# Causal score tiles in pairs, values of 17 columns and second projection buffers in a decoder kernel

## The chip, the cores and the metric

The kernel is one program on one core of a Trainium2 chip. Its time is the device time of one execution in microseconds. Five engines work side by side, each on its own queue of instructions: PE (TensorE, matmuls), DVE (VectorE), ACT (ScalarE), POOL (GpSimd) and SP (SyncE, which issues most DMAs here). "PEld" in the profile is PE's loading of weights.

## The reference, cut to what matters

Four sequences of 512 rows of 256 values go through two decoder layers. Each layer is attention, cross-attention to a context of 1601 rows, and a feed-forward part, each followed by a residual and a layer norm. The second layer is where the change lies: 16 heads of 16 values, causal self-attention with rotated queries and keys, and cross-attention without a mask.

```python
q, k = apply_rope(x @ wq + bq), apply_rope(x @ wk + bk)     # 16 heads of 16
scores = einsum('bnqh,bnkh->bnqk', q, k) / 4
attn = softmax(where(tril, scores, -inf))                   # 512 x 512, causal
x = layernorm(x + einsum('bnqk,bnkh->bnqh', attn, v) @ wo + bo)
x = layernorm(x + cross_attention(x, ctx_512))              # 512 x 1601, no mask
x = layernorm(x + tree_ffn(x))                              # 255 gates, 256 leaves
```

## The kernel before

The program has three stages. `front` makes the first layer's attention and cross-attention, `experts` its sorted mixture of experts, and `heads` the whole second layer. `front` and `experts` end at about 500 us in the profile; the change touches `heads` alone (from line 901 on).

The order of the instructions inside a stage is not written by hand. The stage adds nodes to a `Plan`: each node has an engine, a planned cost, a place in an order (`prio`), the nodes that it depends on, the pool of buffers that it takes one from, and those that it frees. `Plan.run` then picks, over and over, the node that can start earliest by the planned costs, and issues its instructions. So a changed cost or a changed number of buffers moves instructions on every engine, though the chip's own times differ from the planned ones. Matmul nodes carry a mode, `row`, `col` or `full`, and `Plan.turn` tries to keep nodes of one mode together.

In `heads` the work goes by head groups: four heads at a time, four groups per sequence, four sequences, first all of the self-attention and then all of the cross-attention, overlapped by the planner. A group takes these steps:

- `projections` makes queries and keys of eight heads (two groups). For self-attention it also rotates them in `rope`: a product with the rotation matrix, a DVE multiplication into a buffer `rt`, and two POOL operations into `qu` or `ku`. There is one `rt`, one `qu` and one `ku`.
- `apart` copies `qu` and `ku` by eight DMAs into `qT` and `kT`, so that each head lies at its own 32 partitions (lane). A score matmul then uses 32 rows of the array, and four heads can use the four lanes.
- Pass 1 (`score`, `largest`) makes the scores query-major, one tile of 128 queries at a time, and takes each row's maximum on DVE straight out of PSUM. In self-attention tile kq has (kq + 1) x 128 columns, because of the causal mask, and each tile has a PSUM bank of its own (`one`, seven of them).
- The maxima are negated, transposed by PE (`turn`) and added to the queries (`qa`).
- Pass 2 (`score`, `weigh`) makes the scores key-major: key tile t against the queries from t x 128 on. ACT takes Exp from PSUM to an SBUF buffer (`pe`, ten of them); in self-attention POOL then clears the upper triangle (`causal`).
- `product` multiplies by the values, four heads in four column groups of the array, into one bank `acc`. The values `VV` hold 32 columns per head: 16 values, a column of ones that gives the softmax sum, and 15 zeros.

At the start of the stage `begin` gathers the rows that `experts` left in DRAM (four indirect DMAs by POOL for each sequence) and norms them. Before that POOL clears `nm` and `qT` (`clear`), and after the first gathers it writes zeros and ones into `VV` (`ones_behind`). SP meanwhile loads the weights of the tree and fills the three `kT` buffers from `keys0`. The helper `mm` records its matmuls under line 239, so the profile tells the groups apart by their tiles: `one<-kT,qT` is pass 1, `one<-qa,kT` pass 2, and line 1188 the product with the values. Line 1113 is the causal maximum, 1109 that of cross-attention, 1173 Exp, and 1179 the triangle.

Of the kernel before, what the change touches and what calls it, by code (L numbers as in the profile page):

```python
# [29 lines left out]
NS = 31  # L30
NF = 24
# [171 lines left out]
def tile_decoder(ctx: ExitStack, tc: tile.TileContext, a, out):  # L203
# [697 lines left out]
    def heads():  # L901
        plan = Plan()
        with tc.tile_pool(name="h1", bufs=1) as h1, \
# [12 lines left out]
            VV = slots("v", 2, [P, NKT, H // 2, 32])  # L916
# [9 lines left out]
            Q0, RT = slots("q0", 2, [P, L]), slots("rt", 1, [P, L])  # L926
            QU, KU = slots("qu", 1, [P, L]), slots("ku", 1, [P, LC])

            plan.pool("f", 6)
            FF = [*Q0, *RT, junk, *(h1.tile([P, L], F32, tag=f"f{i}", name=f"f{i}") for i in range(2))]  # L930
# [11 lines left out]
            def ones_behind(n, t):  # L942
                nc.gpsimd.memset(t[:, :, :, HD:], 0.0)
                nc.gpsimd.memset(t[:, :, :, HD : HD + 1], 1.0)
# [3 lines left out]

            cleared = N("pool", 1.5, -1.5, clear)
            keyed = [N("dma", 2.5, -4.0, None, [N("sp", 0.4, -4.0, lambda n, k=k: key_rows(n, k))]) for k in range(3)]  # L950
            framed = [N("pool", 5.0, -1.5 + k, lambda n, k=k: ones_behind(n, VV[k])) for k in range(2)]


# [106 lines left out]
            def head_group(cross, b, g, pos, vals, pair, after):  # L1060
# [15 lines left out]
                qd = N("sp", 1.6, pr, lambda n: apart(QT, q, QU, qu, L), [q, cleared, *qs])  # L1076
                qready = N("dma", 0.5, pr, None, [qd], free=[qu])
                kd = N("sp", 1.6, pr, lambda n: apart(KT, k, KU, ku, nk), [k, *keyed, *ks])
# [10 lines left out]
                else:  # L1089
                    for kq in range(4):  # L1090
                        units += [(j, 0, [(kq, 0, (kq + 1) * P)]) for j in range(4)]
                maxes, scored = [], []
                for i, (j, m, prods) in enumerate(units):
                    pu = pos - 1.2 + (i + 0.5) / len(units)
                    js = slice(32 * j, 32 * j + 32)
                    nn, w = len(prods), prods[0][2] - prods[0][1]

                    def score(n, prods=prods, js=js, w=w):
                        for i, (kq, k0, k1) in enumerate(prods):
                            mm(ONE[n.slot][:, i * w : (i + 1) * w], QT[q.slot][js, kq * P : (kq + 1) * P],  # L1100
                               KT[k.slot][js, k0:k1])

                    s = N("pe", cost_mm(nn * w), pu, score, [mx], take=["one"], lanes=(j,), mode="row")

                    def largest(n, s=s, j=j, m=m, prods=prods, w=w):
                        nn, kq = len(prods), prods[0][0]
                        t = ONE[s.slot][:, : nn * w]
                        if cross:
                            nc.vector.tensor_reduce(  # L1109
                                MX[mx.slot][:, kq : kq + nn, j, m : m + 1], t.rearrange("p (a n) -> p a n", a=nn),  # L1110
                                AX.X, ALU.max)
                        else:
                            nc.vector.tensor_tensor_reduce(  # L1113
                                out=junk[:, :w], in0=t, in1=m_qk[:, 384 - kq * P : 512],
                                scale=1.0, scalar=NEG, op0=ALU.add, op1=ALU.max,
                                accum_out=MX[mx.slot][:, kq, j, 0:1])

                    maxes.append(N("dve", dve(nn * w), pu, largest, [s], free=[s]))
                    scored.append(s)
# [38 lines left out]
                for t in range(nkt):  # L1158
                    kn = kt_size(t) if cross else P
                    q0 = 0 if cross else t * P  # L1160
                    exps = []
                    for i, j in enumerate((2, 3, 0, 1)):
                        pu = pos + (t + 0.25 * i) / nkt
                        js = slice(32 * j, 32 * j + 32)
                        w = hold("pe", pu, [acc])
# [349 lines left out]
```

## Time and profile before

| | |
|---|---|
| median of 3 runs | 1765.67 us (1763.68 to 1767.53) |
| profiled execution, its own time | 1755.73 us |
| its span, first to last instruction | 1754.0 us |
| mean granted TensorE clock | 0.967 |
| PE busy, matmuls | 1661.4 us, 10756 records |
| DVE, ACT, POOL busy | 1110.2, 761.5, 342.3 us |

The page gives the busy time of each engine as a share of the span, then the span in 40 slices of 44 us with one digit for each (tenths of the slice), and the granted clock of PE and the load of the DMA engines in the same slices. Below stand the chain of work that ended last, followed back from the last instruction, and the costliest groups of instructions: line, engine, operation, written and read tiles, shape, count, busy time and mean duration. A shape like 32*128 ahead of a matmul's operands is the part of the array that it uses. A matmul in fp32 leaves two records, one for each pass. The profiled execution was 9.94 us shorter than the median of the runs.

### The profile page before, as it was taken

How to read it: one execution, taken by the hardware profiler on the slowest of the kernel's cores; microseconds unless marked ns; L12 is line 12 of the kernel's file. 1: busy time of each engine (PE TensorE's matmuls, PEld its weight loads, DVE VectorE, ACT ScalarE, POOL GpSimd, SP SyncE). 2: the span in 40 equal slices, each digit the busy share in tenths (PEclk: the TensorE clock that was granted, in tenths of full speed). 3: DMA queues.
4: the chain of work that ended last, by engine and by line, in shares of the span. 5: the costliest groups of instructions: out<-in, count | busy, mean ns of one | idle time of the engine just before them, and what ended most of it. 6: DMA issues, size and time to landing. Idle time of an engine off the chain costs nothing.

```text
span 1754.0 us, 28495 instructions
## 1 busy us (share of the span) xinstructions
PE 1661.4 (95%) x10756; PEld 862.5 (49%) x10756; DVE 1110.2 (63%) x2678; ACT 761.5 (43%) x1593; POOL 342.3 (20%) x521
## 2 busy tenths in 40 slices
PE   7899988999968999999999999999999999999995
PEld 4677775887754444454433334433334333343323
DVE  6997654121237766667776666777667776677625
ACT  0335551211112334444355555456554555545581
POOL 6652003432134534442100000100001000010000
PEclk9999987999988989999999999999999999999998
DMA  9000006876431100001100000001000010001000
GB/s 304 29 4 10 13 26 220 290 238 207 144 108 37 32 10 16 13 19 21 24 1 13 14 14 13 1 13 26 13 14 1 13 26 13 14 1 25 1 1 12
DMA packets 40843, 87.50 MB, mean 50 GB/s; under 512 B 7808, under 2 KB 26752, under 8 KB 37632
## 3 DMA queue, kind: packets, MB, share of 16 engines
q1 hardware_dynamic: 31728, 42.58, 9.0%
q0 software_dynamic: 8832, 43.00, 7.1%
q8 instruction: 86, 1.41, 0.3%
q14 instruction: 53, 0.43, 0.1%
q10 hardware_dynamic: 144, 0.07, 0.0%
HBM read 64.52 MB, written 8.26 MB: 41 GB/s over the span
## 4 chain that ended last, share of the span: by engine, by line
PE 83%; DVE 11%; DMA 2%; issue 2%; ACT 1%; POOL 1%; DVEq 0%; POOLq 0%; SPq 0%; ACTq 0%
PE one L239 53%; PE acc L1188 14%; PE e_one L239 11%; DVE junk L1113 1%; PE one L563 1%; PE one L1147 1%; PE one L1208 1%; DMA xs<-x_dram,tok 1%; PE one L1270 1%; DMA y<-ys_dram,dest 1%; DVE sc L423 1%; DVE pm L528 0%; ACT pe L1173 0%; DVE pr L462 0%; DVE qk L406 0%
## 5 line engine op out<-in xcount | busy, mean ns | idle before, releaser
L1173 ACT ACTIVATE pe<-one 128x512 f32<-128x512 f32 (+4 forms) x1088 | 533.0, 566 | 385.9 <-PE one L239 382.1
L1109 DVE TENSOR_REDUCE mx<-one 128x1 f32<-128x512 f32 x768 | 487.7, 683 | 182.1 <-PE one L239 178.3
L239 PE MATMUL one<-qa,kT 32*128 32x512 f32 (+4 forms) x2176 | 512.6, 600 | 7.7 <-ACT pe L1173 6.3
L239 PE MATMUL one<-kT,qT 32*128 32x512 f32 (+4 forms) x2560 | 500.7, 536 | 8.0 <-DVE mx L1113 2.6
L239 PEld LDWEIGHTS one<-qa,kT 32*128 32x128 f32 (+1 forms) x2176 | 171.8, 182 | 227.8 <-issue 78.0
L1188 PE MATMUL acc<-pe,v 128*32 128x512 f32 (+4 forms) x2176 | 270.7, 569 | 0.0
L239 PEld LDWEIGHTS one<-kT,qT 32*128 32x128 f32 x2560 | 191.5, 185 | 153.8 <-ACT pe L1173 45.3
L1276 POOL TENSOR_TENSOR x<-x,rows 128x1024 f32<-128x1024 f32 x12 | 28.3, 2356 | 802.4 <-PE one L1270 802.4
L1113 DVE CUSTOM_DVE_ANT_0 junk<-one,consts 128x256 f32<-128x256 f32 (+3 forms) x256 | 125.4, 490 | 50.7 <-PE one L239 25.8
L1188 PEld LDWEIGHTS acc<-pe,v 128*32 128x32 f32 (+1 forms) x2176 | 43.9, 108 | 178.6 <-issue 161.9
L1179 POOL TENSOR_SCALAR_AFFINE_SELECT pe<-pe 128x128 f32<-128x128 f32 x256 | 72.5, 298 | 140.9 <-ACT pe L1173 137.3
L239 PEld LDWEIGHTS e_one<-xsT,wgu 128*128 128x128 f32 x768 | 90.7, 194 | 4.8 <-issue 3.8
L239 PE MATMUL e_one<-xsT,wgu 128*128 128x128 f32 x768 | 90.6, 277 | 0.0
L239 PE MATMUL e_one<-xT,w_sgu 128*128 128x512 f32 x128 | 61.8, 624 | 3.1 <-DMA w_sgu<-in_w_shared_gu 3.1
L239 PE MATMUL one<-w_in,xT 128*128 128x512 f32 (+1 forms) x128 | 49.5, 543 | 10.4 <-DMA xT<-in_xT 10.4
L243 ACT COPY o<-acc 128x512 f32<-128x512 f32 x32 | 18.7, 586 | 75.5 <-PE acc L1188 75.5
L239 PE MATMUL one<-ctxT,q 128*128 128x512 f32 (+1 forms) x128 | 49.5, 518 | 0.0
L544 ACT ACTIVATE pe<-one,nm 128x512 f32<-128x512 f32 x64 | 37.3, 596 | 27.8 <-DVE nm L536 27.7
L239 PE MATMUL one<-pT,ctxN 128*128 128x128 f32 (+1 forms) x416 | 49.0, 275 | 0.0
L239 PEld LDWEIGHTS one<-pT,ctxN 128*128 128x128 f32 (+1 forms) x416 | 48.2, 192 | 1.6 <-issue 1.2
L852 DVE TENSOR_TENSOR he<-sg,e_one 128x512 f32<-128x512 f32 x24 | 16.5, 686 | 50.7 <-PE e_one L239 48.1
L830 DVE TENSOR_SCALAR xs<-xs,scs 128x256 f32<-128x256 f32 x24 | 8.5, 364 | 60.3 <-DMA xs<-x_dram,tok 60.3
(261 smaller groups left out, 1866.2 us busy)
## 6 DMA issues: line engine op xcount, KB each, us to landing
kT<-ku SPq DMA_DIRECT2D x64, 100.1 KB, 3.4
qT<-qu SPq DMA_DIRECT2D x128, 32.0 KB, 1.9
ctxN<-in_ctxN SPq DMA_DIRECT2D x4, 832.0 KB, 8.9
ctxT<-in_ctxT SPq DMA_DIRECT2D x4, 800.5 KB, 9.5
ys_dram<-ye SPq DMA_DIRECT2D x24, 128.0 KB, 2.4
kT<-in_keys SPq DMA_DIRECT2D x3, 800.5 KB, 9.7
xT<-in_xT SPq DMA_DIRECT2D x16, 128.0 KB, 3.6
x<-in_x SPq DMA_DIRECT2D x16, 128.0 KB, 6.0
```

Source lines behind the costliest of these rows:

```text
L239: nc.tensor.matmul(out, lhsT, rhs, start=c == 0, stop=c == n - 1)
L243: nc.scalar.copy(dst, src)
L423: scores.append(N("dve", 1.21, pos + 0.22 + 0.05 * s, lambda n, s=s, pr=pr: nc.vector.tensor_reduce(SC[sc.slot][:, s].rearrange("p t h -> ...
L544: nc.scalar.activation(PE_[w.slot][:, : k1 - k0], ONE[b.slot][:, : k1 - k0], AF.Exp, bias=NM[nm.slot][:, 1:2], accum_out=PS[sm_.slot][:, i ...
L563: nc.tensor.transpose(ONE[n.slot][:kn, (t % 4) * P : (t % 4 + 1) * P], PE_[w.slot][:, (t % 4) * P : (t % 4) * P + kn], ident)
L1109: nc.vector.tensor_reduce(MX[mx.slot][:, kq : kq + nn, j, m : m + 1], t.rearrange("p (a n) -> p a n", a=nn), AX.X, ALU.max)
L1113: nc.vector.tensor_tensor_reduce(out=junk[:, :w], in0=t, in1=m_qk[:, 384 - kq * P : 512], scale=1.0, scalar=NEG, op0=ALU.add, op1=ALU.max, ...
L1147: nc.tensor.transpose(ONE[n.slot][:, kq * P : (kq + 1) * P], NM[nm.slot][:, kq].rearrange("p j r -> p (j r)"), ident)
L1173: nc.scalar.activation(PE_[w.slot][:kn, q0:], ONE[s.slot][:kn, q0:], AF.Exp, scale=HD**-0.5)
L1179: nc.gpsimd.affine_select(d, d, pattern=[[1, P]], compare_op=ALU.is_ge, fill=0.0, base=0, channel_multiplier=-1)
L1188: nc.tensor.matmul(ACC[acc.slot][32 * j : 32 * j + 32, q0:], VV[v.slot][:kn, t, 4 * (g % 2) + j, :], PE_[exps[j ^ 2][0].slot][:kn, q0:], s ...
L1276: rw = N("pool", pool(1024), pos, lambda n: nc.gpsimd.tensor_tensor(XB[b], XB[b], rows[:, row : row + D].unsqueeze(1).to_broadcast([P, 4, ...
```

## The change

Four things are edited, all in `heads`.

- In self-attention two score tiles go into one PSUM bank. Pass 1 takes the query tiles in the order 3, then 0 and 2 together (128 + 384 columns), then 1. Pass 2 takes the key tiles in the order 0, then 1 and 3 together (384 + 128 columns), then 2. One Exp reads both tiles of a bank and writes one `pe` buffer; the maxima and the triangles are still taken tile by tile.
- The values have 17 columns per head instead of 32, and the product writes 17 partitions of each column group. `acc` is cleared once by DVE at the start of the stage, and POOL no longer writes zeros into `VV`.
- `rt`, `qu` and `ku` have two buffers each. The tree's pool `f` keeps its six buffers: the second `rt` takes the place of one.
- `clear` and `ones_behind` depend on the four gathers of the first sequence. The planned cost of `apart` on SP is 2.7 instead of 1.6, that of `ones_behind` 0.4 instead of 5.0.

```diff
 NS = 31
+MQ = (3,), (0, 2), (1,)
+TQ = (0,), (1, 3), (2,)
 NF = 24
...
-            VV = slots("v", 2, [P, NKT, H // 2, 32])
+            VV = slots("v", 2, [P, NKT, H // 2, HD + 1])
...
-            Q0, RT = slots("q0", 2, [P, L]), slots("rt", 1, [P, L])
-            QU, KU = slots("qu", 1, [P, L]), slots("ku", 1, [P, LC])
+            Q0, RT = slots("q0", 2, [P, L]), slots("rt", 2, [P, L])
+            QU, KU = slots("qu", 2, [P, L]), slots("ku", 2, [P, LC])
 
             plan.pool("f", 6)
-            FF = [*Q0, *RT, junk, *(h1.tile([P, L], F32, tag=f"f{i}", name=f"f{i}") for i in range(2))]
+            FF = [*Q0, *RT, junk, h1.tile([P, L], F32, tag="f0", name="f0")]
...
             def ones_behind(n, t):
-                nc.gpsimd.memset(t[:, :, :, HD:], 0.0)
                 nc.gpsimd.memset(t[:, :, :, HD : HD + 1], 1.0)
 
             def key_rows(n, k):
                 nc.sync.dma_start(KT[k], a["keys0"])
-
-            cleared = N("pool", 1.5, -1.5, clear)
-            keyed = [N("dma", 2.5, -4.0, None, [N("sp", 0.4, -4.0, lambda n, k=k: key_rows(n, k))]) for k in range(3)]
-            framed = [N("pool", 5.0, -1.5 + k, lambda n, k=k: ones_behind(n, VV[k])) for k in range(2)]
 
 
...
-                qd = N("sp", 1.6, pr, lambda n: apart(QT, q, QU, qu, L), [q, cleared, *qs])
+                qd = N("sp", 2.7, pr, lambda n: apart(QT, q, QU, qu, L), [q, cleared, *qs])
                 qready = N("dma", 0.5, pr, None, [qd], free=[qu])
-                kd = N("sp", 1.6, pr, lambda n: apart(KT, k, KU, ku, nk), [k, *keyed, *ks])
+                kd = N("sp", 2.7, pr, lambda n: apart(KT, k, KU, ku, nk), [k, *keyed, *ks])
                 kready = [N("dma", 1.3 if cross else 0.5, pr, None, [kd], free=[ku])]
...
                         kq, m = divmod(n_, 3)
                         units += [(j, m, [(kq, m * 512, m * 512 + 512)]) for j in range(4)]
                 else:
-                    for kq in range(4):
-                        units += [(j, 0, [(kq, 0, (kq + 1) * P)]) for j in range(4)]
+                    for kqs in MQ:
+                        units += [(j, 0, [(kq, 0, (kq + 1) * P) for kq in kqs]) for j in range(4)]
                 maxes, scored = [], []
                 for i, (j, m, prods) in enumerate(units):
                     pu = pos - 1.2 + (i + 0.5) / len(units)
                     js = slice(32 * j, 32 * j + 32)
-                    nn, w = len(prods), prods[0][2] - prods[0][1]
-
-                    def score(n, prods=prods, js=js, w=w):
-                        for i, (kq, k0, k1) in enumerate(prods):
-                            mm(ONE[n.slot][:, i * w : (i + 1) * w], QT[q.slot][js, kq * P : (kq + 1) * P],
-                               KT[k.slot][js, k0:k1])
-
-                    s = N("pe", cost_mm(nn * w), pu, score, [mx], take=["one"], lanes=(j,), mode="row")
-
-                    def largest(n, s=s, j=j, m=m, prods=prods, w=w):
-                        nn, kq = len(prods), prods[0][0]
-                        t = ONE[s.slot][:, : nn * w]
-                        if cross:
-                            nc.vector.tensor_reduce(
-                                MX[mx.slot][:, kq : kq + nn, j, m : m + 1], t.rearrange("p (a n) -> p a n", a=nn),
-                                AX.X, ALU.max)
-                        else:
-                            nc.vector.tensor_tensor_reduce(
-                                out=junk[:, :w], in0=t, in1=m_qk[:, 384 - kq * P : 512],
-                                scale=1.0, scalar=NEG, op0=ALU.add, op1=ALU.max,
-                                accum_out=MX[mx.slot][:, kq, j, 0:1])
-
-                    maxes.append(N("dve", dve(nn * w), pu, largest, [s], free=[s]))
+                    at, w = [], 0
+                    for kq, k0, k1 in prods:
+                        at.append((kq, k0, k1, w))
+                        w += k1 - k0
+
+                    def score(n, at=at, js=js):
+                        for kq, k0, k1, w in at:
+                            mm(ONE[n.slot][:, w : w + k1 - k0], QT[q.slot][js, kq * P : (kq + 1) * P], KT[k.slot][js, k0:k1])
+
+                    s = N("pe", cost_mm(w), pu, score, [mx], take=["one"], lanes=(j,), mode="row")
+
+                    def largest(n, s=s, j=j, m=m, at=at):
+                        for kq, k0, k1, w in at:
+                            t = ONE[s.slot][:, w : w + k1 - k0]
+                            if cross:
+                                nc.vector.tensor_reduce(MX[mx.slot][:, kq, j, m : m + 1], t, AX.X, ALU.max)
+                            else:
+                                nc.vector.tensor_tensor_reduce(
+                                    out=junk[:, : k1 - k0], in0=t, in1=m_qk[:, 384 - kq * P : 512],
+                                    scale=1.0, scalar=NEG, op0=ALU.add, op1=ALU.max,
+                                    accum_out=MX[mx.slot][:, kq, j, 0:1])
+
+                    maxes.append(N("dve", sum(dve(k1 - k0) for _, k0, k1 in prods), pu, largest, [s], free=[s]))
                     scored.append(s)
                 if cross:
...
                 acc = hold("acc", pos, [shifted])
                 o = hold("o", pos, [shifted])
                 last = []
-                for t in range(nkt):
-                    kn = kt_size(t) if cross else P
-                    q0 = 0 if cross else t * P
+                turns = [[t] for t in range(nkt)] if cross else TQ
+                for u, ts in enumerate(turns):
+
+                    at, w = [], 0
+                    for t in ts:
+                        at.append((t, kt_size(t) if cross else P, 0 if cross else t * P, w))
+                        w += L - at[-1][2]
                     exps = []
                     for i, j in enumerate((2, 3, 0, 1)):
-                        pu = pos + (t + 0.25 * i) / nkt
+                        pu = pos + (u + 0.25 * i) / len(turns)
                         js = slice(32 * j, 32 * j + 32)
-                        w = hold("pe", pu, [acc])
-
-                        def score(n, t=t, kn=kn, q0=q0, js=js):
-                            mm(ONE[n.slot][:kn, q0:], KT[k.slot][js, t * P : t * P + kn], QA[qa.slot][js, q0:])
-
-                        s = N("pe", cost_mm(L - q0), pu, score, [w, o, *kready], take=["one"], lanes=(j,), mode="row")
-
-                        def weigh(n, s=s, w=w, kn=kn, q0=q0):
-                            nc.scalar.activation(PE_[w.slot][:kn, q0:], ONE[s.slot][:kn, q0:], AF.Exp, scale=HD**-0.5)
-
-                        r = N("act", act(L - q0), pu, weigh, [s], free=[s])
+                        e = hold("pe", pu, [acc])
+
+                        def score(n, at=at, js=js):
+                            for t, kn, q0, w in at:
+                                mm(ONE[n.slot][:kn, w : w + L - q0], KT[k.slot][js, t * P : t * P + kn], QA[qa.slot][js, q0:])
+
+                        s = N("pe", cost_mm(w), pu, score, [e, o, *kready], take=["one"], lanes=(j,), mode="row")
+
+                        def weigh(n, s=s, e=e, kn=at[0][1], w=w):
+                            nc.scalar.activation(PE_[e.slot][:kn, :w], ONE[s.slot][:kn, :w], AF.Exp, scale=HD**-0.5)
+
+                        r = N("act", act(w), pu, weigh, [s], free=[s])
                         if not cross:
-                            def causal(n, w=w, q0=q0):
-                                d = PE_[w.slot][:, q0 : q0 + P]
-                                nc.gpsimd.affine_select(
-                                    d, d, pattern=[[1, P]], compare_op=ALU.is_ge, fill=0.0,
-                                    base=0, channel_multiplier=-1)
-
-                            r = N("pool", pool(128), pu, causal, [r])
-                        exps.append((w, r))
-
-                    def product(n, t=t, kn=kn, q0=q0, exps=exps):
-                        for j in range(4):
-                            nc.tensor.matmul(
-                                ACC[acc.slot][32 * j : 32 * j + 32, q0:],
-                                VV[v.slot][:kn, t, 4 * (g % 2) + j, :],
-                                PE_[exps[j ^ 2][0].slot][:kn, q0:],
-                                start=t == 0, stop=t == nkt - 1,
-                            )
+                            def causal(n, e=e, at=at):
+                                for t, kn, q0, w in at:
+                                    d = PE_[e.slot][:, w : w + P]
+                                    nc.gpsimd.affine_select(
+                                        d, d, pattern=[[1, P]], compare_op=ALU.is_ge, fill=0.0,
+                                        base=0, channel_multiplier=-1)
+
+                            r = N("pool", len(at) * pool(128), pu, causal, [r])
+                        exps.append((e, r))
+
+                    def product(n, at=at, exps=exps, u=u):
+                        for t, kn, q0, w in at:
+                            for j in range(4):
+                                nc.tensor.matmul(
+                                    ACC[acc.slot][32 * j : 32 * j + HD + 1, q0:],
+                                    VV[v.slot][:kn, t, 4 * (g % 2) + j, :],
+                                    PE_[exps[j ^ 2][0].slot][:kn, w : w + L - q0],
+                                    start=t == 0, stop=u == len(turns) - 1 and t == at[-1][0],
+                                )
                     pr_ = last[-1:] if last else []
-                    last.append(N("pe", cost_mm(L - q0) + 0.05, pos + (t + 1.2) / nkt, product,
-                                  [r for _, r in exps] + vready + pr_, free=[w for w, _ in exps], mode="col"))
+                    last.append(N("pe", cost_mm(w) + 0.05 * len(at), pos + (u + 1.2) / len(turns), product,
+                                  [r for _, r in exps] + vready + [emptied] + pr_, free=[x for x, _ in exps], mode="col"))
                 plan.frees(last[-1], [k, qa])
                 if g % 2:
                     plan.frees(last[-1], [v])
...
+                    if b == 0:
+                        gathered.append(g)
...
+            gathered = []
             done = [begin(b, 4.0 * b - 5.0) for b in range(NB)]
+            cleared = N("pool", 1.5, -1.5, clear, gathered)
+            emptied = N("dve", 0.6, -4.9, lambda n: nc.vector.memset(ACC[0], 0.0))
+            keyed = [N("dma", 2.5, -4.0, None, [N("sp", 0.4, -4.0, lambda n, k=k: key_rows(n, k))]) for k in range(3)]
+            framed = [N("pool", 0.4, -1.5 + k, lambda n, k=k: ones_behind(n, VV[k]), gathered) for k in range(2)]
```

## The prediction

> **What bounds the kernel.** I read the page from the top: engines, slices, the chain of waits.
>
> ```profile
> PE 1661.4 (95%) x10756; PEld 862.5 (49%) x10756; DVE 1110.2 (63%) x2678; ACT 761.5 (43%) x1593; POOL 342.3 (20%) x521
> ...
> PE   7899988999968999999999999999999999999995
> ...
> PEclk9999987999988989999999999999999999999998
> ...
> PE 83%; DVE 11%; DMA 2%; issue 2%; ACT 1%; POOL 1%; DVEq 0%; POOLq 0%; SPq 0%; ACTq 0%
> ```
>
> PE is busy nearly everywhere and makes 83% of the chain. The change touches only the last stage, `heads`, from about 500 us on. The windows of that stage (PE, PEld, DVE, ACT, POOL busy, granted clock) separate its parts: start, self attention, cross attention.
>
> ```profile
> 500.00:545.00 45.00, 24.99 (x95) 14.84 (x95) 24.70 (x62) 6.17 (x10) 26.93 (x26) 0.80 0.39 126
> 545.00:835.00 290.00, 283.72 (x1910) 141.21 (x1910) 207.35 (x749) 117.30 (x290) 116.25 (x272) 0.94 0.08 19
> 905.00:1700.00 795.00, 789.74 (x5542) 298.69 (x5540) 546.05 (x1056) 445.60 (x850) 27.36 (x55) 1.00 0.06 12
> ```
>
> The start has 20 us of idle PE. In self and cross attention no other engine is over 72%. But "busy" is a union over four lanes, so the timeline of PE must say what its time is made of:
>
> ```profile
> 913.23 0.70 PE L239 MATMUL one<-qa,kT 32*128 32x512 f32 x3
> 913.25 0.69 PE L239 MATMUL one<-kT,qT 32*128 32x512 f32 x1
> 913.76 0.60 PE L239 MATMUL one<-qa,kT 32*128 32x512 f32 x3
> 913.78 1.00 PE L239 MATMUL one<-kT,qT 32*128 32x512 f32 x3
> 914.21 0.59 PE L239 MATMUL one<-qa,kT 32*128 32x512 f32 x1
> ...
> 1110.78 0.59 PE L239 MATMUL one<-kT,qT 32*128 32x512 f32 x1
> 1111.30 1.06 PE L1188 MATMUL acc<-pe,v 128*32 128x512 f32 x8
> 1112.29 0.71 PE L239 MATMUL one<-kT,qT 32*128 32x512 f32 x4
> ```
>
> Every matmul is two records (passes). Four lanes start 7 ns apart and run side by side. One pass of 512 columns holds its lane 0.43 us (913.78 to 914.21, both on lane 0), so a matmul of n columns takes n x 1.667 ns. The first pass in a lane is 0.69 us, later ones 0.59: 0.105 us of weight load show once per run of equal mode, none after it. At a change of mode (32-row scores, 32-column products, full) PE stands 0.09 us: 1110.78 + 0.43 = 1111.21, and the product starts at 1111.30. The median of all such gaps is 0.091 to 0.096 us.
>
> So I counted the instruction order of both programs in `heads` (4304 matmuls each) and priced it with these rows: longest lane of each run, one gap and one first load per run. Before, this gives 1108 us of the 1246 us from 508 us to the end; group by group it follows the trace (head groups 10 to 15 of self attention: 16.6, 14.5, 14.4, 20.7, 16.4, 20.0 counted; 16.7, 16.8, 15.4, 20.1, 16.4, 21.7 between the ends of their products). PE's own order is therefore the term to work out. The other 138 us are waits, most of them in score runs.
>
> **The change, part by part.**
>
> *Shared banks (MQ, TQ).* The matmuls stay (same numbers of the same shapes); their order does not. From the two orders:
> - runs of one mode: scores 404 to 387, products 267 to 254, full 184 to 179. Prices: 17 x (0.093 + 0.106) = 3.4; 13 x (0.093 + 0.026) = 1.5; 5 x (0.093 + 0.105) = 1.0. Together -5.9 us.
> - the longest lanes of the score runs, added up: 477.1 to 468.6 us, -8.5 us (the full and product streams stay at 265.3 and 211.6).
>
> This counts the two tiles of a bank, which follow each other on one lane, as if the other lanes ran on beside them. The weight loads of the stretch above are the evidence:
>
> ```profile
> 913.76 0.18 PEld L239 LDWEIGHTS one<-kT,qT 32*128 32x128 f32 x1 [0.23 <-issue]
> 913.78 0.18 PEld L239 LDWEIGHTS one<-qa,kT 32*128 32x128 f32 x1
> ```
>
> In program order the `qa` score of lane 0 stands ahead of the `kT` score of lane 1. Lane 0 came free 20 ns later, and lane 1's load and then its matmul (914.19 against 914.21) went ahead. Likewise the first passes of lanes 2, 3 and 0 (to 913.25) go ahead of lane 1's second pass (913.76), which stands before them. A waiting lane does not hold the next one; I take that for pairs too, though there up to three passes wait on a lane where this row shows one or two.
>
> [...]
>
> *Other engines under the pairs.* Exp on 512 columns takes 0.603 us against 0.287 + 0.513 for 128 and 384: 64 x 0.197 = 12.6 us less ACT, hidden (117 of 290 busy). The causal selects stay 256 (0.298 us each), but a product now waits for two per lane: one Exp and eight selects, some 3 us, against a counted 7.0 us median of PE work between the pair's last score and its product (5.1 before for 384 columns; least 2.6). Covered, or about 0.5 us where it is not. The reductions stay 16 per group. Seven more PSUM copies (0.68 us) and one tree's levels go to DVE, which is 69% busy in cross attention: 0, at most +5 if it were late.
>
> *Bank turns.* A self-attention group fills 24 banks instead of 32. In the self window PE's weight loads waited:
>
> ```profile
> PEld one L239 <- DVE mx L1113: 24.3, 48, 3.2
> PEld one L239 <- ACT pe L1173: 19.8, 36, 0.8
> ```
>
> A quarter fewer turns would take a quarter of 44.1, -11 us, if all of it stopped PE; against it, a bank is held for two reductions, 64 banks each 0.45 us longer (a 128-column reduction to the next), +29 us if each were waited for, about +3 at the rate of the row (48 waits in 512 turns, one in ten). I take -2, nearer to the rate.
>
> *Values of 17 columns.* A product's first pass lasts 617 ns, its second 592: 25 ns for 32 columns of weights, as 105 ns for 128. 17 columns: 13 ns. 254 runs x 12.5 ns = -3.2 us. Below: the 108 ns loads of second passes are hidden already. The added memset of ACC is one DVE instruction (about 0.6 us, as a 512-column ACT copy) first in its queue; the y adds behind it wait for gathers until 511.58 anyway, after 13.45 us of idle DVE. If it waited for a bank until then: +0.6.
>
> *Clears behind the gathers.* Here the start is set by POOL:
>
> ```profile
> 502.31 0.99 POOL L940 MEMSET nm<- 128x512 f32 x2 [33.90 <-DMA ys_dram<-ye]
> 503.24 0.99 POOL L940 MEMSET qT<- 128x512 f32 x2
> 504.39 0.96 POOL L1319 DMA_INDIRECT y<-ys_dram,dest  x1 [0.16 <-issue]
> ```
>
> The gathers feed the first norm, the first projections and all that follows. Ahead of the clears they issue 504.39 - 502.31 = 2.1 us earlier; they wait for the same ys_dram stores. The clears land in POOL's 6.5 us of idle time before 519.13, where 3.6 us of VV memsets shrink to 0.55. On SP the four tree weights now go ahead of the first key rows (0.34 us), which no score needs before 540. Bounds: 0, if the landing (6 us, queued with 3.4 MB of loads) does not move; -5, if the gathers also miss part of that queue. Taken: -2.
>
> *Second rt, qu, ku.* Before, k's rotation waited for q's rt: `ku` was complete at 536.8, 6.7 us behind `qu` (530.0). In the new order both projections stand together and DVE's second rt product is ahead of the norm chain. Bounds 0 and -4 (first scores at 540.6; PE then still waits for DVE); taken -2. Elsewhere it only moves projections earlier, which the count above holds. SP's planned 2.7 us for four copies changes no instruction; they take 2.4 us, and their number stays 271.
>
> Sum: -5.9 - 8.5 - 3.2 - 2 - 2 - 2 = -23.6 us. The profiled execution took 1755.7 us (span 1754.0), so 1732; it was 9.9 us under the median 1765.67. Against that median: 1742.
>
> **Rivals.**
>
> *Lanes wait in order* (slower). If lane j+1 cannot start before both tiles of lane j have started, four lanes of the pair (1, 3) take 4 x 0.64 + 0.106 + 0.21 = 2.88 us instead of 0.96, and those of (0, 2) 4 x 0.213 + 0.106 + 0.64 = 1.60: +2.56 us a group, +41 us over 16 groups. 1742 + 41 = 1783. It decides as soon as more than 0.6 of the penalty is paid (23.6/41). The overtaking rows speak against it; that they show one waiting matmul, not a pair, for it. Chance 0.12.
>
> *PE's saving comes back as waiting.* If evacuations, not PE's order, set the pace, counted PE time does not shorten the run; only start-up remains, with a few us of the rest: -2 to -10, 1756 to 1764. For it: 128 us of waiting in score runs. Against: the counts follow the trace group by group. Chance 0.18, half of it inside 0.2%.
>
> *Shared banks hold PE up.* The +29 us end in place of -2: 1742 + 31 = 1773. Against: one turn in ten waited, 0.5 us each. Chance 0.04; small spills of it, with Exp and selects late, 0.02 inside 0.2%.
>
> **The numbers.** Forecast 0.64, all of it faster. 0.2% (3.5 us) is about what a measurement of this kernel can tell. Faster: 0.64 + 0.09 = 0.73, same 0.09 + 0.02 = 0.11, slower 0.12 + 0.04 = 0.16. Low end: -17.6 - 5 - 4 - 11 = -37.6, 1728, and 5 us below it for the clock (0.94 granted in self attention, 3 us a hundredth if it rises with less idling): 1723. The high end takes in the second rival and the edge of no change: 1768. About 0.2 stays outside: the slow rivals and the low tail.
>
> **What would show it.** Right: 820 runs of one mode; the four 384-column scores of a pair start 7 ns apart in the timeline, not 0.6 us; first passes of products near 605 ns; the first gather at about 502.3; self-attention groups some 0.6 us shorter on average; weight loads there waiting no longer than now for the maxima and Exp. Wrong: staggered starts within pairs (first rival), or weight loads waiting over 44 us for evacuations in self attention, or a cross stage unchanged in spite of 8 fewer runs.

## The result, and the profile after

The changed kernel took 1748.76 us (median of 4 runs, 1738.24 to 1749.57) against 1764.68 us (1763.14 to 1767.53): ratio 0.9894, 95% interval 0.9854 to 0.9934. In a second session it was 1744.57 against 1761.37 us, ratio 0.9913 (0.9883 to 0.9943). So it is about 16 us faster, where 23.6 us were forecast; the time lies in the forecast's range, 1723 to 1768 us, 7 us above its centre of 1742. Its profiled execution took 1748.63 us (span 1746.9).

The page's engines, slices of the granted clock, and chain of waits:

```profile
PE 1656.4 (95%) x10756; PEld 864.5 (49%) x10756; DVE 1102.3 (63%) x2689; ACT 760.1 (44%) x1535; POOL 329.6 (19%) x503
...
PEclk9999988999988999998999999999999999999998
...
PE 65%; DVE 4%; ACT 1%; issue 1%; DMA 1%; POOL 0%; DVEq 0%; ACTq 0%
```

PE's share is what it was. The chain's shares add up to 72% here, so it could not be followed as far back as before, and nothing below rests on it. The windows of `heads` (columns as before: PE, PEld, DVE, ACT, POOL, granted clock):

```profile
500.00:545.00 45.00, 31.26 (x110) 18.84 (x112) 26.17 (x75) 7.01 (x12) 25.30 (x27) 0.75 0.39 126
545.00:835.00 290.00, 283.40 (x1960) 146.46 (x1960) 211.60 (x755) 116.10 (x238) 113.35 (x278) 0.96 0.09 20
905.00:1700.00 795.00, 788.08 (x5542) 293.20 (x5538) 536.18 (x1052) 451.01 (x860) 19.55 (x38) 0.99 0.06 12
```

PE is busy 6 us longer in the same 45 us of the start, at a lower clock (0.75 against 0.80), and the self window gets 50 more matmul passes through. The cross window gets through the same 5542, at a clock of 0.99 in place of 1.00.

With the forecast's prices for PE's order, each stage of the two profiled executions splits into counted work, clock (half of the time in which the clock stood at half speed, whether PE was busy or not) and a rest, which is put down to waiting. In cross attention little of that rest is an idle PE, since PE's records cover 788 of the 795 us of the window, while its weight loads of scores waited 90.1 us for the maxima and 89.2 us for Exp there: by my estimate from these numbers, most of the rest is runs that last longer than their longest lane, one lane waiting while another runs. The stages end with the last products of a head group:

| us | before: time = work + clock + rest | after: time = work + clock + rest |
|---|---|---|
| start, 502 us to the end of the first head group | 70.4 = 35.8 + 13.7 + 21.0 | 74.6 = 43.1 + 17.1 + 14.4 |
| other 15 groups of self attention | 298.8 = 269.9 + 11.9 + 17.0 | 283.3 = 259.9 + 5.1 + 18.3 |
| 16 groups of cross attention | 842.3 = 785.5 + 1.7 + 55.0 | 846.3 = 770.8 + 11.9 + 63.6 |
| tail | 40.6 = 16.6 + 7.6 + 16.4 | 40.8 = 16.6 + 7.9 + 16.3 |

The gain lies in the start (7.3 us more work for 4.2 us more time) and in self attention. Cross attention has 14.7 us less work and is no shorter: the clock took 10.2 us and waiting 8.6. These two executions differ by only 7.1 us, since the one of before was 9 us under its median. The next table therefore uses all runs.

**Two shares of the time.** Each run lists its span and mean granted clock. Span x clock is taken as the span at full clock ("full-clock time"); the rest of the span is called lost to the clock. That is a way of keeping accounts: a time in which PE would wait for another engine anyway counts as lost too when the clock is low in it. Means over the runs, against the kernel before on the same chip; below about 4 us they say little, and two rows of this table, same_again and clears_first, turned out to run the same instructions and still differ by 4.1 us in the last column. "Counted" is the PE work of `heads` against the changed kernel's 1090.4 us.

| kernel | median us (runs) | ratio to before, 95% | counted | full-clock time | lost to the clock |
|---|---|---|---|---|---|
| changed (same_again) | 1744.57 (6) | 0.9913, 0.9883-0.9943 | 0 | -10.7 | -3.3 |
| no_pairs | 1756.16 (12) | 0.9971, 0.9951-0.9992 | +8.6 | -3.0 | -0.9 |
| pairs_pass1 | 1760.68 (12) | 1.0009, 0.9986-1.0033 | +3.9 | +6.6 | -5.2 |
| pairs_pass2 | 1757.61 (12) | 0.9978, 0.9956-1.0000 | +4.1 | -9.0 | +6.2 |
| cols32 | 1748.48 (6) | 0.9909, 0.9881-0.9936 | +3.3 | -6.8 | -10.0 |
| clears_first | 1745.29 (6) | 0.9901, 0.9868-0.9933 | 0 | -10.5 | -7.4 |
| onebuf | 1780.29 (6) | 1.0083, 1.0057-1.0109 | +4.0 | -2.8 | +17.7 |
| one_rt | 1765.41 (12) | 1.0007, 0.9992-1.0021 | -0.6 | -5.1 | +7.1 |
| one_qk | 1774.13 (7) | 1.0053, 1.0035-1.0071 | +2.8 | -9.8 | +20.0 |
| copies16 | 1758.34 (12) | 0.9975, 0.9956-0.9993 | +1.5 | -9.6 | +3.2 |
| z_b4_a16 | 1739.67 (6) | 0.9863, 0.9842-0.9883 | -11.4 | -10.0 | -13.4 |
| z_b12_a24 | 1895.63 (6) | 1.0746, 1.0712-1.0780 | -55.7 | +105.4 | +26.9 |

Differences between two rows are differences of ratios times 1763 us, uncertain by about 0.004 (6 to 7 us).

### The profile page after: what moved, and what is told of

It is laid out like the page before. It is cut to its first block, busy times and chain, and to the rows that moved or that the text cites. A ratio compares the mean times of both kernels' runs of the same rounds, so it can differ in the third digit from the quotient of the medians.

```text
span 1746.9 us, 28364 instructions
## 1 busy us (share of the span) xinstructions
PE 1656.4 (95%) x10756; PEld 864.5 (49%) x10756; DVE 1102.3 (63%) x2689; ACT 760.1 (44%) x1535; POOL 329.6 (19%) x503
## 4 chain that ended last, share of the span: by engine, by line
PE 65%; DVE 4%; ACT 1%; issue 1%; DMA 1%; POOL 0%; DVEq 0%; ACTq 0%
PE one L241 47%; PE acc L1192 14%; DVE junk L1110 1%; PE one L1212 1%; PE one L1144 1%; PE one L1274 1%; ACT pe L1175 1%; DMA y<-ys_dram,dest 1%; PE one L1293 0%; DVE x L1259 0%; DVE lst L1251 0%; DVE y L1310 0%; DVE lsd L1241 0%; POOL y L1323 0%; DVE rt L1372 0%
## 5 line engine op out<-in xcount | busy, mean ns | idle before, releaser
L1175 ACT ACTIVATE pe<-one 128x512 f32<-128x512 f32 (+2 forms) x1024 | 526.9, 592 | 414.0 <-PE one L241 411.6
L241 PE MATMUL one<-qa,kT 32*128 32x512 f32 (+4 forms) x2176 | 518.4, 600 | 6.1 <-ACT pe L1175 4.9
L241 PEld LDWEIGHTS one<-qa,kT 32*128 32x128 f32 (+1 forms) x2176 | 180.3, 182 | 205.5 <-issue 70.1
L1192 PE MATMUL acc<-pe,v 128*17 128x512 f32 (+4 forms) x2176 | 267.9, 569 | 0.0
L1110 DVE CUSTOM_DVE_ANT_0 junk<-one,consts 128x128 f32<-128x128 f32 (+3 forms) x256 | 125.2, 489 | 38.4 <-PE one L241 15.1
L1192 PEld LDWEIGHTS acc<-pe,v 128*17 128x17 f32 (+1 forms) x2176 | 38.3, 96 | 178.7 <-issue 164.5
L1182 POOL TENSOR_SCALAR_AFFINE_SELECT pe<-pe 128x128 f32<-128x128 f32 x256 | 68.2, 293 | 135.7 <-ACT pe L1175 134.9
L854 DVE TENSOR_TENSOR he<-sg,e_one 128x512 f32<-128x512 f32 x24 | 16.4, 685 | 50.3 <-PE e_one L241 47.7
L241 PE MATMUL e_one<-wdn,he 128*128 128x256 f32 x192 | 45.6, 380 | 0.8 <-DVE he L854 0.7
```

What stands on the lines that cost most here:

```text
L241: nc.tensor.matmul(out, lhsT, rhs, start=c == 0, stop=c == n - 1)
L854: h = N("dve", dve(512), pr, lambda n, s=s, p=banks[1], he=he: nc.vector.tensor_tensor(HE[he.slot].rearrange("p j t -> p (j t)"), SG[s.slo ...
L1110: nc.vector.tensor_tensor_reduce(out=junk[:, : k1 - k0], in0=t, in1=m_qk[:, 384 - kq * P : 512], scale=1.0, scalar=NEG, op0=ALU.add, op1=A ...
L1175: nc.scalar.activation(PE_[e.slot][:kn, :w], ONE[s.slot][:kn, :w], AF.Exp, scale=HD**-0.5)
L1182: nc.gpsimd.affine_select(d, d, pattern=[[1, P]], compare_op=ALU.is_ge, fill=0.0, base=0, channel_multiplier=-1)
L1192: nc.tensor.matmul(ACC[acc.slot][32 * j : 32 * j + HD + 1, q0:], VV[v.slot][:kn, t, 4 * (g % 2) + j, :], PE_[exps[j ^ 2][0].slot][:kn, w : ...
```

## The experiments

All start from the changed kernel.

**same_again**: the changed kernel, no edit.

> The changed kernel once more, as the control that the three kernels beside it are compared with. Theory and rivals alike: 0.990 of the kernel before, about 16 us less, as in its first runs. Should it come out at -24 us or at -7 us, the first four runs had been a poor sample, and all the terms below have to be held against the new number.

Measured 0.9913: as expected.

**no_pairs**:

```diff
-MQ = (3,), (0, 2), (1,)
-TQ = (0,), (1, 3), (2,)
+MQ = (0,), (1,), (2,), (3,)
+TQ = (0,), (1,), (2,), (3,)
```

> Undoes the shared banks alone: MQ and TQ hold one tile each, in the order of before; the values of 17 columns, the second buffers and the clears stay. Theory (the counted PE order is the time): 853 runs of one mode in place of 820, 1099.0 us of counted PE work in place of 1090.4, so 8.6 us slower than the changed kernel beside it. Rival (what PE saves comes back as waiting): within 3 us of it, with the waits of scores for banks and reductions making up the difference. Rival (shared banks hold PE up): faster than it.

11.6 us slower than same_again on the same chip, 7.7 of it at full clock against 8.6 counted. The shared banks do what the count said, and neither rival holds.

**pairs_pass1** and **pairs_pass2**:

```diff
-TQ = (0,), (1, 3), (2,)
+TQ = (0,), (1,), (2,), (3,)
```
```diff
-MQ = (3,), (0, 2), (1,)
+MQ = (0,), (1,), (2,), (3,)
```

> Keeps the pair (0, 2) of the maxima's pass and undoes the pair (1, 3) of the second pass. Theory: 839 runs, 1094.3 us counted, so 3.9 us slower than the changed kernel beside it. Rival (the second pass waits for a longer Exp and two selects per lane, which the forecast put at nothing): faster than the changed kernel, by up to 3 us. Rival (all comes back as waiting): no difference.

> Keeps the pair (1, 3) of the second pass and undoes the pair (0, 2) of the maxima's pass. Theory: 827 runs, 1094.5 us counted, so 4.1 us slower than the changed kernel beside it. Rival (a bank held for two reductions holds PE up, the term of bank turns): faster than the changed kernel, by some 3 us or more. Rival (all comes back as waiting): no difference.

Both are far slower than counted, 16.1 and 13.0 us, and for different reasons. In pairs_pass1 all of it is full-clock time (17.3 us more than same_again). Waits of PE's weight loads from 502 to 905 us (total, times, longest), for the causal selects, of pairs_pass1 and then of the changed kernel:

```profile
PEld acc L1192 <- POOL pe L1182: 15.1, 28, 1.4
```
```profile
PEld acc L1192 <- POOL pe L1182: 3.8, 7, 0.8
```

The forecast feared that a pair's product waits for two selects per lane. The opposite is seen: the unpaired products of pairs_pass1 wait for their selects four times as often as the paired ones of the changed kernel. But unpaired tiles alone do not do it: the same row has 5.9 us and 13 waits before and 9.0 us and 19 waits in no_pairs, whose second passes are unpaired too. So the 11.3 us belong to this run's order as well. PE itself stood idle for these selects for only 1.7 us (5 times), so it is not shown how much of the 17.3 they are. In pairs_pass2 full-clock time is only 1.7 us above same_again; the clock lost 9.5 us more. In the profiled execution one half-speed stretch of 20.5 us, from 857.2 us on, makes 10.2 us of its loss (more on it under one_qk). That the two halves cost more than no_pairs, which undoes both, means that their prices don't add.

**cols32**:

```diff
-VV = slots("v", 2, [P, NKT, H // 2, HD + 1])
+VW = slots("v", 2, [P, NKT * (H // 2) * (HD + 1) + 15])
...
-ACC[acc.slot][32 * j : 32 * j + HD + 1, q0:],
-VV[v.slot][:kn, t, 4 * (g % 2) + j, :],
+ACC[acc.slot][32 * j : 32 * j + 32, q0:],
+VW[v.slot][:kn, (8 * t + 4 * (g % 2) + j) * (HD + 1) : (8 * t + 4 * (g % 2) + j) * (HD + 1) + 32],
```

> Undoes the 17 columns alone: a product again loads 32 columns of weights, read from the same 17-column rows (the last 15 are the next head's values and land in rows of the accumulator that nobody reads); the order of the instructions is that of the changed kernel, and one memset more stands on GpSimd. Theory: each of 254 product runs begins with a load of 25 ns in place of 13 ns, so 3.3 us slower than the changed kernel (about -12.6 us against before). Rival (the first load is not on the path): within 1 us of the changed kernel.

The step is confirmed, not its worth. The first 512-column pass of a product in cross attention lasts 0.617 us here and 0.604 in the changed kernel (medians of 196 and 198); full-clock time is 3.9 us more than in same_again and 3.7 more than in clears_first on the same chip, against 3.3 counted. But the ratio, 0.9909, is that of the changed kernel: the clock lost 6.7 us less than in same_again and 2.6 less than in clears_first, and the second of these is within the noise.

**clears_first**: `cleared` stands ahead of the gathers again and waits for none of them.

```diff
+            cleared = N("pool", 1.5, -1.5, clear)
...
-            cleared = N("pool", 1.5, -1.5, clear, gathered)
```

> Puts the clears of nm and qT back ahead of the first gathers; the PE order stays. Theory: the first gather issues 2.1 us later and the whole start moves with it: 2 us slower than the changed kernel. Rival (the landing of the gathered rows is set by the queue of loads, not by the issue): no difference. Upper bound of the forecast: 5 us slower.

The edit does not do what it was to do. POOL's first rows in `heads`, of the changed kernel and then of clears_first:

```profile
502.81 0.94 POOL L1323 DMA_INDIRECT y<-ys_dram,dest  x1 [34.56 <-DVE acc L1407]
...
507.49 1.01 POOL L942 MEMSET nm<- 128x512 f32 x2
```
```profile
504.25 0.95 POOL L1323 DMA_INDIRECT y<-ys_dram,dest  x1 [34.55 <-DVE acc L1407]
...
508.96 1.00 POOL L942 MEMSET nm<- 128x512 f32 x2
```

In both the clears stand behind the four gathers: without the dependence the planner still puts them there, and every engine gets the same instructions in the same order. clears_first is the changed kernel once more (0.9901 against 0.9913), and no run undoes the clears. That its first gather comes 1.4 us later has nothing to do with them: the last product of `experts` ends 1.4 us later too (500.69 against 499.25 us), in a part of the program that is the same in all kernels. The run is of use as the changed kernel on the chip of cols32 and onebuf.

**onebuf**, then **one_rt** (the first and last line of the edit) and **one_qk** (the middle line):

```diff
-slots("rt", 2, [P, L])
+slots("rt", 1, [P, L])
-QU, KU = slots("qu", 2, [P, L]), slots("ku", 2, [P, LC])
+QU, KU = slots("qu", 1, [P, L]), slots("ku", 1, [P, LC])
-FF = [*Q0, *RT, junk, h1.tile([P, L], F32, tag="f0", name="f0")]
+FF = [*Q0, *RT, junk, *(h1.tile([P, L], F32, tag=f"f{i}", name=f"f{i}") for i in range(2))]
```

> Takes the second rt, qu and ku away again and gives the second spare frame back. Theory: 817 runs, 1094.4 us counted in place of 1090.4, and some 2 us of waiting at the start: 4 to 6 us slower than the changed kernel. Rival (the buffers were never waited for once the first scores run): only what the start shows, 0 to 2 us slower.

30 us slower than same_again (1.0083 against 0.9913) and 32 us slower than clears_first on the same chip (0.9901), far outside both expectations, and slower than the kernel before. 7.9 us is full-clock time, about what was expected; 21.0 us is the clock (7.7 and 25.1 against clears_first).

> Taking away all three second buffers cost 35 us, of which the lost clock was 25. This kernel takes away the second rt alone (and gives the frame back); qu and ku stay double. Counted PE work 1089.8 us in place of 1090.4 and 817 runs. Theory (the half-speed slices follow from PE's waits, and q's and k's rotations wait for each other only where they share rt): within 4 us of the changed kernel. Rival (the shared rt is what the 35 us came from): 1770 us or more.

> The complement: the second qu and ku go, rt stays double. Counted 1093.2 us, 819 runs. Theory (a projection that waits for the four copies of the group before it stops PE, and a half-speed slice of 3.4 us follows): 1760 to 1780 us, with the lost clock nearer to 86 us than to 62. Rival (the rt): 1745 to 1752 us. Rival (PE order alone): 3 us slower than the changed kernel.

one_rt: 17 us slower, between the two expectations. one_qk: 25 us slower, with 87.3 us lost to the clock where the changed kernel loses 61.6; that theory's numbers hold. Nearly all of one_qk is clock: full-clock time is 0.9 us more. The theory's mechanism, projections that wait for the copies and stop PE, is not shown. In the profiled executions one half-speed stretch where self attention ends, 17.1 us long in onebuf (from 873.0 us) and 20.5 in one_qk (from 865.5), makes 8.5 and 10.2 us of the lost clock; the changed kernel has none over 10.2 us after 545 us. In the slice of 3.4 us ahead of it PE runs scores of 65 key columns and is 85% (onebuf) and 90% busy; within it PE's records cover all of the time, so no wait of PE explains its length. That stays open.

The second `rt` shows at the start. DVE's two products with the rotated rows, of the changed kernel and of one_rt:

```profile
525.98 0.69 DVE L1012 TENSOR_TENSOR rt<-one,consts 128x512 f32<-128x512 f32 x1 [1.41 <-PE one L241]
...
528.63 0.69 DVE L1012 TENSOR_TENSOR rt<-one,consts 128x512 f32<-128x512 f32 x1 [0.51 <-PE one L241]
```
```profile
527.89 0.69 DVE L1012 TENSOR_TENSOR rt<-one,consts 128x512 f32<-128x512 f32 x1 [2.23 <-PE one L241]
...
534.54 0.69 DVE L1012 TENSOR_TENSOR rt<-one,consts 128x512 f32<-128x512 f32 x1
```

With one buffer the second product comes 6.7 us after the first, behind the norm chain on DVE; with two, 2.7 us. First scores start at 539.08 in one_rt (540.57 before), at 535.71 in the changed kernel and 534.17 in one_qk. The last product of `experts` ends between 496.9 and 504.4 us in the profiled executions; counted from there, first scores come after 41.2 us before, 38.3 in one_rt, 43.3 in onebuf and 34.6 to 36.8 in all others. The rest (waiting) of the start is 21.0, 21.4 and 22.2 us in the profiles of before, one_rt and onebuf, and 11.7 to 18.4 in those of the changed kernel and of all others but z_b12_a24.

**copies16**:

```diff
-qd = N("sp", 2.7, pr, lambda n: apart(QT, q, QU, qu, L), [q, cleared, *qs])
+qd = N("sp", 1.6, pr, lambda n: apart(QT, q, QU, qu, L), [q, cleared, *qs])
```

and `kd` likewise.

> The changed kernel with SP's four copies planned at 1.6 us again, as before; not one instruction is added or left out, the planner only puts them in another order: 801 runs, 1091.9 us counted (1.5 more). It measures what a re-planning by itself is worth. Theory (counted work, waits and clock): within 5 us either way. Rival (the order is so finely balanced that any re-planning costs 10 us or more): 1755 us or more; then single edits of this study say little below 10 us.

11 us slower (0.9975 against 0.9913; the intervals don't meet): the rival, though its profiled execution, at 1745.31 us its fastest, does not show it. The same work in another planned order is worth as much as the shared banks. It is not quite the same instructions: the planner also gives one tree back to POOL (503 to 519 instructions there, 2689 to 2672 on DVE). By the means over the runs, full-clock time is 1.1 us more and the clock's loss 6.5; where in the stage this lies is not shown.

**z_b12_a24** and **z_b4_a16**, each one added line at the head of `heads`:

```diff
+        plan.BURST, plan.AWAY, plan.IDLE = 12, 2.4, 1.0
```
```diff
+        plan.BURST, plan.AWAY, plan.IDLE = 4, 1.6, 0.5
```

> The changed kernel with three constants of the planner set for the heads stage (longest burst of one mode, cost of leaving a mode, idle time it accepts for staying), so that PE stays longer in one mode: 600 runs in place of 820, 1034.7 us counted in place of 1090.4; the same instructions otherwise. Theory (counted PE order is the time): up to 56 us faster than the changed kernel, about 1693 us. Rival (waits set the pace and PE's saving comes back): less than a fifth of it, 1740 us or more, since longer bursts ask for banks faster than the reductions and Exps empty them; the windows then show the rest that is not PE work grow from 113 us to some 160 us.

> A mild form of the longer stay in one mode: the longest burst stays as it is, only the time away from scores that is accepted goes from 0.8 to 1.6: 722 runs in place of 820, 1079.0 us counted, 11.4 less, nearly all of it in self attention and in full and product streams. Theory of the forecast (counted order): 11 us faster than the changed kernel, 1735 us. Rival (as with the long bursts, which lost 151 us: scores come late, banks fill late, reductions and Exps run dry): slower than the changed kernel, with the rest that is not PE work up by more than 11 us. From the long bursts' result I hold the second for likelier.

z_b12_a24 takes 55.7 us off the counted work and is some 150 us slower. Its rest is 288.0 us against 112.6, more than that rival's 160. Weight loads of scores waiting for Exp in cross attention (905 to 1700 us), z_b12_a24 and then the changed kernel:

```profile
PEld one L241 <- ACT pe L1176: 117.4, 302, 2.3
```
```profile
PEld one L241 <- ACT pe L1175: 89.2, 138, 1.6
```

Long bursts wait for Exp more than twice as often. That is the rival's sign, but these waits grew by 28 us in this window and 43 over the whole of cross attention (94.7 to 138.1), and the rest by 175; what makes up the others is not shown. So counted work is not the time once its order asks more of the other engines.

z_b4_a16 is the fastest kernel of the study: 0.9863 of before, 7 to 9 us under the changed kernel (0.9901 and 0.9913), close to the theory's number. But not by its mechanism: the rest grew by 10.8 us, which is the rival's and eats the 11.4 counted; full-clock time did not move (-10.0 against -10.7), and the clock lost 6 to 10 us less. Both theories are half right.

## Why the prediction was right or wrong

Direction and range were right, and of the mechanism the counted order held where one part was undone. That the total came within 8 us of the sum is in part luck: waiting and clock took back most of what was forecast for cross attention, the second buffers and the planned copies were worth far more than their terms, and the worth of the clears was not measured.

**Lanes overtake.** Right, and the slower rival falls. A whole pair (1, 3) in the second pass, four lanes x two tiles x two passes, on PE's timeline:

```profile
582.24 1.17 PE L241 MATMUL one<-qa,kT 32*128 32x384 f32 x16
583.34 0.66 PE L1144 MATMUL one<-consts,nm 128*128 128x128 f32 x4
```

From the first start to the next kind of matmul 1.10 us, near the 0.96 plus a mode change that the count has; waiting in order would have taken 2.88. The four 384-column tiles start 13 ns apart (7 were forecast, 0.6 us feared). Only 2 of the 16 groups show all four starting together (within 0.04 us); in the others the starts are spread out.

**The counted order.** 820 runs of one mode, and right as a price where one part was undone: 7.7 us at full clock for the banks (8.6 counted), 3.7 to 3.9 for the 17 columns (3.3). As the price of the whole stage it held in self attention (8.7 us of 10.0 at full clock; a group is 1.0 us shorter, 0.6 were forecast) and not in cross attention: 6.2 of 14.7. There the second rival, PE's saving coming back as waiting, is right. The forecast listed a cross stage unchanged as a sign against it, and that sign is in the table. Its reason against this rival, that counts followed the trace group by group, came from groups of self attention alone.

**Bank turns.** Right in sign. The self window that the forecast read (560 to 835 us) now shows

```profile
PEld one L241 <- DVE mx L1110: 29.0, 57, 1.1
PEld one L241 <- ACT pe L1175: 9.7, 17, 1.3
```

38.7 us in place of 44.1: Exp's half fell, the maxima's rose. The third rival falls.

**Second buffers: mis-sized.** Forecast -2 us, at the start alone. The start's rest fell by 6.6 us (all parts of the change together), and undoing the buffers costs 30 us. The step that failed is "Elsewhere it only moves projections earlier, which the count above holds".

**Planned copies: mis-sized.** Forecast nothing, since "SP's planned 2.7 us for four copies changes no instruction". It changes their order; undone, 11 us.

**Clears: not measured.** Forecast -2 us, from a first gather 2.1 us earlier. Counted from the last product of `experts`, it comes after 3.56 us in the changed kernel and 4.99 before (499.40 to 504.39), so 1.4 us earlier, and the first product of the norm after 18.57 in place of 19.51 us. What that is worth at the end no run shows.

**The tree on DVE.** Forecast "0, at most +5 if it were late". It was late. Before, one of the two trees of each pair during cross attention ran on POOL; of the second pair of trees both now run on DVE, from 1341.3 to 1349.7 us, in the third quarter of cross attention, and for 8.3 us DVE takes no maximum between the head groups' scores (longest such stretch before: 6.8). What PE then does, and DVE's next maxima:

```profile
1350.41 1.58 PE L241 MATMUL one<-kT,qT 32*128 32x65 f32 x27 [2.61 <-DVE mx L1108]
```
```profile
1349.68 1.88 DVE L1108 TENSOR_REDUCE mx<-one 128x1 f32<-128x512 f32 x3
```

PE waits 2.61 us, and 1.9 us after it starts again the clock drops to half for 6.83 us, another 3.4 us. This quarter of the stage has 5.3 us more rest and 3.4 more clock than before. What the other 3 us of added rest in cross attention wait for is left open.

The drop of the clock is no chance of one execution. In the profiled executions both trees of a pair run on DVE in one go 14 times during cross attention (twice each in no_pairs, pairs_pass1, onebuf and one_qk), and 14 times the clock halves within 3 us of the second tree's end, for 6.8 or 10.2 us. Of the 25 pairs that DVE and POOL share, none is followed so within 10 us. The added rest is another matter: copies16 and z_b4_a16 share this pair between DVE and POOL, and their rest in this quarter is 0.8 us more and 0.3 us less than the changed kernel's.

**No term for the clock.** This is the main failure of the sum: the clock stood in it only as 5 us at the low end of the range. The parts of the change look additive in the counted work, but single undoings cost 12 (banks), 30 (buffers) and 11 us (planned copies) of a gain of 16. In the last two most of that is the clock (by the means 21.0 of 28.9 and 6.5 of 7.6 us), in the first it is not (2.4 of 10.1). The 138 us that the forecast called waits held the clock too: 34.9 us in the table of stages. That each re-planning puts the waits elsewhere, and that the clock answers to where they fall, fits the trees above and the slices at the end; no run tests it by itself.

## What to carry to other kernels

Price PE's order from its own rows, but believe the price only in a stage whose trace follows it; in cross attention, where PE also waits for other engines, 14.7 us less counted work came with 8.6 us more waiting, so read stage by stage. Any edit that a planner sees, even a planned cost (11 us in copies16), is a re-planning and can be worth as much as the edit one means; look into the trace whether the edit moved what it was meant to move. In this kernel, whose PE is busy for 95% of the span, short waits close together were followed by a loss of clock as well (waits of 0.35 to 0.38 us, then half speed for 3.41 us from 560.4 us on), so compare kernels by span x clock as well as by time.

## What the runs showed of the hardware

In the profiled executions the granted clock steps between full and half on a grid of 3.41 us that is fixed within an execution and lies differently in each (the first step down is at 35.66 us before and at 34.79 in the changed kernel). I divided the 14 profiled executions of this case into these slices, from 545 us to the end of the last products, with the time that PE's records cover in each:

| PE busy in a slice at full speed | slices | next slice at half speed |
|---|---|---|
| under 45% | 14 | 14 |
| 45 to 65% | 16 | 11 |
| 65 to 80% | 86 | 44 |
| 80 to 90% | 157 | 20 |
| 90 to 97.5% | 130 | 9 |
| above | 4201 | 4 |

A stretch at half speed lasts two slices on average (206 in 102 stretches), which the accounts above book as a loss of about 3.4 us. Even a full slice at half speed was followed by another in 74 of 177 cases. A slice that was only in part busy, on PE's timeline of the changed kernel, where the clock halves at 560.4 us:

```profile
557.56 0.69 PE L241 MATMUL one<-kT,qT 32*128 32x256 f32 x2 [0.35 <-DVE mx L1110]
558.63 0.69 PE L241 MATMUL one<-kT,qT 32*128 32x256 f32 x2 [0.38 <-DVE mx L1110]
559.67 0.66 PE L1144 MATMUL one<-consts,nm 128*128 128x128 f32 x4 [0.35 <-DVE mx L1110]
560.72 3.52 PE L241 MATMUL one<-xT,wk 128*128 128x512 f32 x4 [0.38 <-DVE mx L1110]
```

Waits of 0.35 to 0.38 us for the maxima, none of them long, leave PE busy for 65% of the slice that ends at 560.4; the four projection passes behind them take 3.52 us where the same four take 1.88 at 531.93. Of the slices with PE 65 to 80% busy, 44 of 86 were followed by one at half speed.

In the runs of same_again and of the kernel before, most of the spread is in the loss to the clock: over the six runs of same_again, full-clock time has a standard deviation of 1.3 us, the loss to the clock 3.4; over 29 runs of the kernel before, 3.0 and 5.8. The phase of the grid, which differs between the profiled executions, may be the reason; that is not shown.
